# A four-layer model on one core: one table of constants, layer-1 weights made beside layer 0, and the first half batch sent ahead

## The chip, the core and the metric

The kernel runs on one core of a Trainium2 chip as one launch. The metric is the device time of one execution in microseconds; lower is better. Six names are used for the engines: PE is TensorE (matrix products into PSUM), DVE is VectorE, ACT is ScalarE, POOL is GpSimd, SP is SyncE, which issues the DMA transfers, and PEld is the weight load of PE.

## The reference

The input is `data`, 4 sequences of 1024 rows with 128 columns, all float32. Four pairs of an attention-like step and a feed-forward step follow one another, eight residual steps in all, and each is closed by a layer normalisation over the 128 columns. The sketch names the steps in the kernel's counting, layer 0 to layer 7.

```
x = data
x = ln(x + concat(x, softplus(count(x) @ W1 + b1)) @ W2)      # layer 0 (count: see below)
x = ln(x + gelu(x @ bin(w1).T + b1) @ bin(w2).T + b2)         # layer 1: bin(w) = row mean of |w| times sign(w)
x = ln(x + attn(x))                                           # layer 2: for each row and head, scores q[i]*k[j] of the row's own
                                                              #   64 channels, causal softmax over j, times v[j]
x = ln(x + ln2(gelu(x @ tern(W_fc).T)) @ tern(W_proj).T)      # layer 3: ternary weights
x = ln(x + gated linear attention along the sequence)         # layer 4
x = ln(x + experts weighed by a sigmoid)                      # layer 5
x = ln(x + chunked state-space scan)                          # layer 6
x = ln(x + two rounds of top-2 of 64 Kronecker experts)       # layer 7
```

In layer 0 the count of a row is the sum over all 1024 rows of its sequence of the positive part of the cosine similarity. Layer 2 has, for every row and each of 16 heads, a 64 by 64 causal softmax: this is most of the work.

## The kernel before, in words

The 4096 rows are cut into 8 blocks of 512 rows (`NG`, `TPG` tiles of 128 rows each); two blocks are one sequence. A block has its rows `x` and its transposed rows `xT`, which the layers update in place.

The instructions are written by Python generators, one for each piece of work. A generator yields the name of the engine on which its next instructions run and what they need (free tiles of some kind, a condition). The class `Order` holds a planned clock for each engine; it always takes the piece that can start first by these clocks, and among pieces within 0.05 us the one with the better rank (`URGE`: closing a unit, then `prepare`, then the chains a, b and c, then the rest, then the feed). The instructions are emitted in that order, and every engine executes its own in that order. The instructions of `start` are ahead of that; on an engine they may change places with the planned ones.

The rooms in SBUF are lists of tiles by kind (`room`): six tiles `a` of 512 columns, one `ha` and one `hc` of 2048 columns, and so on. PSUM has `acc`, two `kvr` and four `bg`.

- `start` loads constants and parameters into one tile `cst`, one transfer for each, the first two blocks of x, the layer-0 weight `w0`, three rows of biases, and `Wo`. From SP's side these are issued one after the other.
- `fold` (rank feed) loads six pieces of the layer-2 weights into tiles `a`, multiplies each on PE with the constant matrix `less`, and copies the result on ACT into `wq` and `wkv`.
- `chain_a` runs `front(0)`, `front(1)`, `ternarise`, and then for each group of tiles the layers 3, 4 and 5, with `front(b + 2)` behind the groups of a block. `front` of an even block runs `layer0` for that block and the next one together; `front(0)` also runs `binarise`, which makes the two layer-1 weights (absolute value on ACT, sums over rows on PE, sign on ACT, three products or sums on DVE) and stores them in DRAM. Then it runs `layer1` for its own block and sets row `ONE` of `xT` to one on POOL. That row carries the biases of layer 2; `ready2` then says that layer 2 may begin on that block.
- `layer0` normalises both blocks into the tile `nT` (kind `ha`); `count` then makes eight similarity products for a block (each block needs `nT` of both), reduces each on ACT, and computes the rest of the layer.
- `layer1` loads both weights from DRAM, makes four projections into a tile `ha`, one GELU (a table load on ACT before and after it), four sums over the hidden columns, and the normalisation.
- `prepare` makes, tile by tile, the queries and the running maxima and minima of the keys, and copies them by DMA into the layouts `qr` and `mr`. `feed` and `rest` are layer 2 itself: for each of 64 units of work 17 ring steps, each of them a product on DVE into a piece of the ring `ringe`, a subtraction on POOL, an exponential on ACT, a sum on PE, another product on DVE and another sum on PE. `close` finishes a unit.
- `chain_b` runs layer 6 and `chain_c` runs layer 7 on the groups that chain a has finished. How far a chain may lag behind the feed is told by `LAG`, in units of the feed's progress.

Of the kernel before, what the change touches and what calls it, by code (L numbers as in the profile page):

```python
# [20 lines left out]
P = 128  # L21
# [8 lines left out]
H, C, R, S, NK = 16, 64, 4, 2, 16  # L30
SH = S * H
ERING = 8768
LUMPS = 8
EPS = 0.05
ONE = 96
LAG = {"chain_a": (0.7, 300), "chain_b": (1.6, 290), "chain_c": (2.6, 132)}

# [248 lines left out]
class Model:  # L286
# [94 lines left out]

    def start(self):
        nc, a = self.nc, self.a
        load = {"ident": P, "rep": P, "SL": P, "U": P, "ex4": P, "ex2": P, "g4": 16, "g2": 32, "su": P, "sd": P, "par": 4, "iota": LUMPS,
                "blk": P, "less": P, "bz": 48, "route": 16, "beyond": R}
        par = {"f0_b1": 4, "f1_lnw": 4, "f1_lnb": 4, "a2_nw": 1, "f2_b1": 16, "f2_Wu": 1, "a0_W1": 1, "a0_b1": 1}
        wide = {"f2_bu": 1, "a3_bdt": 16, "a3_Alog": 16, "f3_sup": 1, "f3_sdn": 1}
        total = sum(load.values()) + sum(par.values()) + sum(wide.values()) + 64 + 32 + 128
        cst = self.keep([P, total], "cst")
        self.k, at = {}, 0  # L390

        def put(name, src, cols, bcast=False, rows=P):
            nonlocal at
            dst = cst[:, at : at + cols]
            self.k[name] = dst
            at += cols
            for r in range(0, P, rows):
                self.d.dma_start(dst[r : r + rows], src.to_broadcast([P, cols]) if bcast else src)

        put("ident", a["c_ident"], P)  # L400
        self.ident = self.k["ident"]
        self.ones = self.keep([P, P], "ones")
        self.v.memset(self.ones, 1.0)
        self.neghalf = self.keep([P, TPG], "neghalf")
        self.v.memset(self.neghalf, -0.5)
        self.eps = self.keep([P, 1], "eps")
        self.v.memset(self.eps, LN_EPS)
        for g in (0, 1):
            self.load_x(g)
        for n, c in par.items():  # L410
            put(n, a[n], c)
        for n, c in load.items():
            if n != "ident":
                put(n, a["c_" + n], c)
        for n, c in wide.items():
            put(n, a[n], c, bcast=True)
        put("bup", a["f3_bup"], 64, rows=64)
        put("bdn", a["f3_bdn"], 32, rows=32)
        put("bd", a["c_bd"], 128)
        self.w0 = self.keep([P, 2, D], "w0")  # L420
        self.d.dma_start(self.w0, a["a0_W2"].rearrange("(c p) d -> p c d", p=P))


        self.bias = self.keep([66, 512], "bias", dtype=BF16)
        self.v.memset(self.bias, 0.0)
        left, part = self.new("a"), self.new("b").bitcast(BF16)[:66, :512]
        self.v.memset(left[:66], 0.0)
        for i in range(3):
            self.d.dma_start(left[32 * i : 32 * i + 2], a["bias"])
        for i in range(3):  # L430
            self.v.tensor_copy(part, left[:66])
            self.v.tensor_copy(self.bias[32 * i : 32 * i + 2], part[32 * i : 32 * i + 2])
            self.v.tensor_tensor(left[:66], left[:66], part, ALU.subtract)
        self.drop(left, part)
        self.pick = self.keep([66, 2], "pick", dtype=BF16)
        self.v.tensor_copy(self.pick, self.k["rep"][:66, :2])
        self.Wo = self.keep([P, 8, D], "Wo")
        self.d.dma_start(self.Wo, a["a1_Wo"].rearrange("(c p) d -> p c d", p=P))
        self.lo0 = self.keep([P, 8, C], "lo0")
        self.g.memset(self.lo0, 0.0)  # L440
        self.g.memset(self.lo0[:, :, 0:1], -BIG)
        self.ering = Ring(self.keep([P, ERING], "ringe"), ERING)
        self.state = self.keep([P, H, 8], "state")
        self.last = self.keep([P, 8], "last")
        self.negA = self.keep([P, H], "negA")
        self.s.activation(self.negA, self.k["a3_Alog"], AF.Exp)
        self.v.tensor_scalar_mul(self.negA, self.negA, -1.0)

        self.ident16 = self.keep([P, P], "ident16", dtype=BF16)
        self.v.tensor_copy(self.ident16, self.ident)  # L450
        self.mask16 = self.keep([P, P], "mask16", dtype=BF16)
        self.v.tensor_scalar(self.mask16, self.k["SL"], -30000.0, None, ALU.mult)
        self.nbu = self.keep([P, 1], "nbu")
        self.v.tensor_scalar_mul(self.nbu, self.k["f2_bu"], -1.0)
# [150 lines left out]
        yield from self.norm(g, "a%d" % (g.k % 2), po)  # L605

    def layer0(self, b):
        gs = self.blocks[2 * b : 2 * b + 2]
        for g in gs:
            if g.x is None:  # L610
                yield "SP", self.free("x")
                self.load_x(g.k)
            yield "ACT", self.free("xT")
            g.xT = self.new("xT")
        yield "ACT", self.free("ha")
        nT = self.new("ha")
        yield from self.together(*(self.normalise(g, nT) for g in gs))
        yield from self.together(*(self.count(g, nT) for g in gs))
        self.drop(nT)


    def binarise(self):

        self.w1 = []
        for half, n, count in ((0, 1, D), (1, 4, 512)):
            src = self.a["f0_w1T"] if half == 0 else self.a["f0_w2T"].rearrange("(c p) d -> p c d", p=P)
            wT = yield from self.load("a", src, *((512,) if half == 0 else (4, D)))
            wT = wT if half == 0 else wT.rearrange("p c d -> p (c d)")
            cols = 512 // n
            yield "ACT", self.free("a", 3)  # L630
            ab, bw, alpha = self.new("a"), self.new("a"), self.new("a")
            self.s.activation(ab, wT, AF.Abs)
            yield "PE", self.free("bg")
            pa = self.new("bg")
            for i in range(n):
                self.pe.matmul(
                    pa[:, :cols], lhsT=self.ones, rhs=ab[:, i * cols : (i + 1) * cols], start=(i == 0), stop=(i == n - 1)
                )
            yield "ACT"
            self.s.activation(alpha[:, :cols], pa[:, :cols], AF.Copy, scale=1.0 / count)  # L640
            self.s.activation(bw, wT, AF.Sign)
            self.drop(pa)
            yield "DVE"
            for i in range(n):
                s = slice(i * cols, (i + 1) * cols)
                self.v.tensor_tensor(bw[:, s], bw[:, s], alpha[:, :cols], ALU.mult)
            self.v.tensor_tensor(bw, bw, wT, ALU.subtract)
            self.v.tensor_tensor(wT, wT, bw, ALU.add)
            self.drop(ab, bw, alpha)
            yield "SP"  # L650
            self.w1.append(self.keep([P, 512], "w1", pool=self.dram))
            self.d.dma_start(self.w1[half], wT)
            self.drop(wT)

    def project(self, out, lhsT, rhs, bias):
# [1053 lines left out]

    def front(self, b):  # L1710
        if b.k % 2 == 0:
            yield from self.layer0(b.k // 2)
        if b.k == 0:
            yield from self.binarise()
        yield from self.layer1(b)
        yield "POOL"
        self.g.memset(b.xT[ONE : ONE + 1], 1.0)
        self.ready2 = b.k + 1
# [59 lines left out]
    def run(self):  # L1778
# [13 lines left out]
        with self.tc.manual_schedule():  # L1792
            self.log_exp()
            self.order.spawn(self.fold(), "feed")
            self.order.spawn(self.prepare(), "prepare")
            for chain in (self.chain_a, self.chain_b, self.chain_c):
                self.order.spawn(chain(), chain.__name__)
            self.order.spawn(self.feed(), "feed")
            self.order.run()
# [13 lines left out]
def arrays_of(i):  # L1813
    f = {k: np.asarray(v) for k, v in i.items()}
    c = np.ascontiguousarray
    row = lambda v: c(np.reshape(v, (1, -1)))
    cols = lambda v: c(np.reshape(v, (-1, P)).T)
    a = {
        "x": c(f["L0_attn_data"].reshape(NB * SEQ, D)),
        "a0_W1": cols(f["L0_attn_W1"]),  # L1820
        "a0_b1": cols(f["L0_attn_b1"]),
        "a0_W2": f["L0_attn_W2"],
        "f0_w1T": c(f["L0_ffn_w1"].T),
        "f0_w2T": c(f["L0_ffn_w2"].T),
        "f0_b1": cols(f["L0_ffn_b1"]),
        "a1_Wo": f["L1_attn_Wo"],
# [50 lines left out]
    for n, s in (("up", "up"), ("dn", "down")):  # L1877
# [5 lines left out]
    p, q = np.arange(P)[:, None], np.arange(P)[None, :]  # L1883
# [1 line left out]
        "ident": p == q,  # L1885
        "SL": p > q,
        "U": p <= q,
        "rep": p % 32 == q % 32,
        "blk": (p % 16 == q % 16) / 8.0,
        "less": ((p == q) * 1.0 - (p == ONE)) * (q != ONE),  # L1890
        "bz": np.pad(p // 8 == np.arange(16)[None, :], ((0, 0), (16, 16))) * 8**-0.5,
# [9 lines left out]
        "par": np.concatenate([p // n % 2 == np.arange(2)[None, :] for n in (4, 2)], 1) * LUMPS,  # L1901
        "iota": np.arange(LUMPS)[None, :] + 0 * p,
    }
    a.update({"c_" + n: c(np.asarray(v, np.float32)) for n, v in k.items()})
    return a


# [15 lines left out]
```

## Time and profile before

| | |
|---|---|
| time, median of 3 runs (lowest, highest) | 4459.69 us (4457.38, 4463.85) |
| profiled execution, own time | 4459.83 us |
| its span, first to last instruction | 4458.1 us |
| mean granted PE clock | 0.875 |
| DVE busy | 3637.0 us, 82% of the span |
| PE busy | 3532.0 us, 79% |
| POOL busy | 2697.3 us, 61% |
| ACT busy | 2443.8 us, 55% |

The busy times are sums over instructions, and what an engine waits for comes from the events of the semaphores. Nearly every instruction of this kernel is recorded by one helper, so that they all have the line L52; they are told apart by their tiles. In the order of time, a row has the start, the time (of one instruction or of several alike that are merged, with their number behind an x), the engine, the operation, the tile written and those read, and in brackets how long the engine had been idle and what ended that. `SPq` is a transfer's issue on SP's queue. In the table by stage a row has the stretch and its length, the busy time (and number of instructions) of PE, PEld, DVE, ACT and POOL, the granted PE clock, the DMA engines' mean busy share, and GB/s. In the table of waits the numbers are the sum in us, how often, and the longest.

### The profile page before, as it was taken

The page shows a single profiled execution, that of the slowest core. Times are in us where ns is not written, and L with a number is a line of the kernel's source. Part 1 is how long each engine was busy: PE and PEld are TensorE (multiplying, and loading weights), DVE is VectorE, ACT ScalarE, POOL GpSimd, SP SyncE. Part 2 cuts the span into 40 slices and gives each one's busy share as a digit, 9 for nine tenths or more (in the row PEclk, how much of TensorE's full clock was granted, in tenths as well). Part 3 has the DMA queues.
Part 4 walks back from the last instruction along what each step waited for, and adds up shares of the span by engine and source line. Part 5 has one row for each costly group of instructions (what it writes and reads, how often), then busy time and mean ns, then how long its engine had stood idle before and what let it go on. Part 6 is the DMA issues. An engine that isn't in the chain of part 4 may idle for free.

```text
span 4458.1 us, 91232 instructions
## 1 busy us (share of the span) xinstructions
PE 3532.0 (79%) x37044; PEld 1856.1 (42%) x37044; DVE 3637.0 (82%) x5143; ACT 2443.8 (55%) x4083; POOL 2697.3 (61%) x1254
## 2 busy tenths in 40 slices
PE   4567677788788888888788888988788888879973
PEld 2222224344344434444354434544354434437762
DVE  2899999899888998879979998779989998883421
ACT  3455555766446755657555655657555654555520
POOL 0598866776567775567756766557666775560111
PEclk8788889988899989989899888999998988998976
DMA  1221212212223232222323333133323223331555
GB/s 52 67 57 39 47 42 61 50 44 50 58 65 79 73 95 67 67 72 67 96 64 86 77 87 84 38 84 87 89 60 96 67 74 86 77 89 34 142 153 124
DMA packets 389933, 328.12 MB, mean 74 GB/s; under 512 B 201660, under 2 KB 325372, under 8 KB 389512
## 3 DMA queue, kind: packets, MB, share of 16 engines
q1 hardware_dynamic: 379016, 288.73, 26.3%
q0 software_dynamic: 10496, 33.56, 2.6%
q8 instruction: 290, 4.75, 0.5%
q14 instruction: 131, 1.07, 0.1%
HBM read 147.05 MB, written 40.89 MB: 42 GB/s over the span
## 4 chain that ended last, share of the span: by engine, by line
DVE 37%; PE 31%; issue 12%; POOL 9%; ACT 9%; DMA 2%; SPq 1%; DVEq 0%; POOLq 0%; ACTq 0%
DVE ringe L52 23%; PE bg L52 18%; PE acc L52 10%; POOL ringe L52 9%; DVE bg L52 5%; ACT ringe L52 4%; PE kvr L52 3%; SPq L52 1%; DVE a L52 1%; DVE x L52 1%; ACT ha L52 1%; DVE b L52 1%; DVE ast L52 1%; DVE t L52 1%; ACT b L52 1%
## 5 line engine op out<-in xcount | busy, mean ns | idle before, releaser
L52 POOL TENSOR_TENSOR ringe<-ringe,mr 128x1024 f32<-128x1024 f32 (+14 forms) x1088 | 2548.7, 2380 | 1150.5 <-DVE ringe L52 789.9
L52 PE MATMUL acc<-ringe,cst 128*32 128x256 f32 (+6 forms) x17418 | 1370.6, 428 | 509.2 <-ACT ringe L52 244.3
L52 ACT ACTIVATE ringe<-ringe 128x256 f32<-128x256 f32 (+14 forms) x962 | 997.6, 1053 | 790.2 <-POOL ringe L52 788.1
L52 DVE TENSOR_TENSOR ringe<-ringe,kvr 128x1024 f32<-128x1024 f32 (+14 forms) x1098 | 1289.8, 1204 | 129.9 <-PE acc L52 108.2
L52 DVE TENSOR_TENSOR ringe<-qr,kvr 128x1024 f32<-128x1024 f32 (+14 forms) x1088 | 1278.4, 1211 | 82.3 <-PE acc L52 45.7
L52 PEld LDWEIGHTS acc<-ringe,cst 128*32 128x32 f32 x17418 | 424.5, 115 | 1230.7 <-DVE ringe L52 467.6
L52 ACT ACTIVATE ringe<-ringe,cst 128x256 f32<-128x256 f32 x512 | 353.5, 771 | 106.7 <-POOL ringe L52 106.1
L52 PE MATMUL bg<-xT,a 128*128 128x512 f32 (+2 forms) x506 | 286.9, 675 | 34.8 <-DVE t L52 11.1
L52 PEld LDWEIGHTS bg<-b,b 64*128 64x128 f32 (+1 forms) x1650 | 178.8, 203 | 101.3 <-issue 42.6
L52 PE MATMUL bg<-b,b 64*128 64x128 f32 (+2 forms) x1650 | 202.2, 290 | 18.9 <-DVE b L52 5.5
L52 PE MATMUL kvr<-wkv,xT 128*32 128x256 f32 x2048 | 157.1, 430 | 48.4 <-DVE ringe L52 48.0
L52 PE MATMUL bg<-a,ha 128*128 128x128 f32 x1168 | 169.5, 291 | 12.8 <-ACT ha L52 12.8
L52 DVE TENSOR_TENSOR_SCAN bg<-lo,bg 128x512 f32<-128x512 f32 x128 | 155.4, 1217 | 22.2 <-ACT bg L52 22.2
L52 ACT COPY b<-bg 128x512 f32<-128x512 f32 (+2 forms) x245 | 106.7, 446 | 121.7 <-PE bg L52 119.8
L52 PEld LDWEIGHTS bg<-a,ha 128*128 128x128 f32 x1168 | 149.9, 201 | 24.9 <-ACT ha L52 14.5
L52 PEld LDWEIGHTS bg<-xT,a 128*128 128x128 f32 (+1 forms) x506 | 92.1, 213 | 159.1 <-issue 62.0
L52 ACT ACTIVATE ha<-bg,cst 128x512 f32<-128x512 f32 (+1 forms) x157 | 102.2, 665 | 79.8 <-PE bg L52 78.2
L52 POOL DMA_INDIRECT c<-in_f_tdn,elumps x22 | 20.8, 943 | 200.4 <-issue 196.0
L52 ACT ACTIVATE bg<-bg 128x512 f32<-128x512 f32 (+3 forms) x176 | 89.2, 509 | 75.8 <-PE bg L52 73.3
L52 ACT ACTIVATE b<-cst,five 128x128 f32<-128x128 f32 x412 | 129.5, 392 | 0.0
L52 DVE TENSOR_TENSOR b<-b,bg 128x256 f32<-128x256 f32 (+3 forms) x272 | 100.9, 401 | 34.0 <-PE bg L52 18.3
L52 PE MATMUL bg<-b,cst 128*128 128x512 f32 (+1 forms) x208 | 113.9, 634 | 0.5 <-ACT b L52 0.4
(598 smaller groups left out, 4641.5 us busy)
## 6 DMA issues: line engine op xcount, KB each, us to landing
qr<-q SPq DMA_DIRECT2D x512, 128.0 KB
mr<-t SPq DMA_DIRECT2D x512, 128.0 KB
a<-in_f_W SPq DMA_DIRECT2D x65, 256.0 KB
c<-in_f_Wdn SPq DMA_DIRECT2D x55, 256.0 KB
tu<-c SPq DMA_DIRECT2D x52, 256.0 KB
c<-tu SPq DMA_DIRECT2D x200, 64.0 KB
c<-td SPq DMA_DIRECT2D x98, 128.0 KB
td<-c SPq DMA_DIRECT2D x47, 256.0 KB
```

The costliest lines, as they stand in the source:

```text
L52: return f(*args, **kw)
```

## The change

- All constants and the small parameters come as one array `cst` that is put together on the host, in the order of `CST`. It is loaded by two transfers: the identity alone, and the other 1475 columns. The two blocks of x are issued ahead of each. The parameters that were spread over the partitions by a broadcasting transfer are repeated in the array. The constant `rep` has 32 columns in place of 128.
- `binarise` is spawned as a task of its own with the rank of chain a, ahead of `prepare` and the chains. Every `front` waits, before `layer1`, until both stored weights are there.
- `layer0(0)` normalises both blocks into a tile `hc`, runs `count` for block 0 alone, and hands the tile on. `front(0)` then goes to `layer1`. `front(1)` runs `count` for block 1 with that tile, gives it back, and goes to `layer1`. For later pairs `layer0` does both blocks together as before, in `ha`.

```diff
+CST = {
+    "ident": P, "a0_W1": 1, "a0_b1": 1, "f0_b1": 4, "f1_lnw": 4, "f1_lnb": 4, "a2_nw": 1, "f2_b1": 16, "f2_Wu": 1,
+    "f2_bu": 1, "a3_bdt": 16, "a3_Alog": 16, "f3_sup": 1, "f3_sdn": 1, "bup": 64, "bdn": 32, "rep": 32, "SL": P, "U": P,
+    "ex4": P, "ex2": P, "g4": 16, "g2": 32, "su": P, "sd": P, "par": 4, "iota": LUMPS, "blk": P, "less": P, "bz": 48,
+    "route": 16, "beyond": R, "bd": P,
+}
...
     def start(self):
...
-        def put(name, src, cols, bcast=False, rows=P):
-            nonlocal at
-            dst = cst[:, at : at + cols]
-            self.k[name] = dst
+        cst = self.keep([P, sum(CST.values())], "cst")
+        self.k, at = {}, 0
+        for name, cols in CST.items():
+            self.k[name] = cst[:, at : at + cols]
             at += cols
-            for r in range(0, P, rows):
-                self.d.dma_start(dst[r : r + rows], src.to_broadcast([P, cols]) if bcast else src)
-
-        put("ident", a["c_ident"], P)
+        self.load_x(0)
+        self.d.dma_start(cst[:, :P], a["cst"][:, :P])
+        self.load_x(1)
+        self.d.dma_start(cst[:, P:], a["cst"][:, P:])
...
-        for g in (0, 1):
-            self.load_x(g)
-        for n, c in par.items():
-            put(n, a[n], c)
-        for n, c in load.items():
-            if n != "ident":
-                put(n, a["c_" + n], c)
-        for n, c in wide.items():
-            put(n, a[n], c, bcast=True)
-        put("bup", a["f3_bup"], 64, rows=64)
-        put("bdn", a["f3_bdn"], 32, rows=32)
-        put("bd", a["c_bd"], 128)
...
     def layer0(self, b):
+
+        room = "ha" if b else "hc"
...
-        yield "ACT", self.free("ha")
-        nT = self.new("ha")
+        yield "ACT", self.free(room)
+        nT = self.new(room)
         yield from self.together(*(self.normalise(g, nT) for g in gs))
+        if b == 0:
+            yield from self.count(gs[0], nT)
+            return nT
         yield from self.together(*(self.count(g, nT) for g in gs))
         self.drop(nT)
...
     def binarise(self):
 
-        self.w1 = []
...
-            self.w1.append(self.keep([P, 512], "w1", pool=self.dram))
-            self.d.dma_start(self.w1[half], wT)
+            put_by = self.keep([P, 512], "w1", pool=self.dram)
+            self.d.dma_start(put_by, wT)
+            self.w1.append(put_by)
             self.drop(wT)
...
     def front(self, b):
         if b.k % 2 == 0:
-            yield from self.layer0(b.k // 2)
-        if b.k == 0:
-            yield from self.binarise()
+            self.nT = yield from self.layer0(b.k // 2)
+        elif b.k == 1:
+            yield from self.count(b, self.nT)
+            self.drop(self.nT)
+        yield "SP", self.when(lambda: len(self.w1) == 2)
         yield from self.layer1(b)
...
             self.order.spawn(self.fold(), "feed")
+            self.w1 = []
+            self.order.spawn(self.binarise(), "chain_a")
             self.order.spawn(self.prepare(), "prepare")
```

On the host, `arrays_of` puts the constants and parameters together into `cst` and passes the single arrays no more.

More of the change, by code (lines that the diff above doesn't have):

```diff
@@ L383, in start @@
         nc, a = self.nc, self.a
[L384 to L389, printed above, removed]
+        cst = self.keep([P, sum(CST.values())], "cst")
         self.k, at = {}, 0
-        def put(name, src, cols, bcast=False, rows=P):
-            nonlocal at
-            dst = cst[:, at : at + cols]
-            self.k[name] = dst
+        for name, cols in CST.items():
+            self.k[name] = cst[:, at : at + cols]
             at += cols
-            for r in range(0, P, rows):
-                self.d.dma_start(dst[r : r + rows], src.to_broadcast([P, cols]) if bcast else src)
-        put("ident", a["c_ident"], P)
+        self.load_x(0)
+        self.d.dma_start(cst[:, :P], a["cst"][:, :P])
+        self.load_x(1)
+        self.d.dma_start(cst[:, P:], a["cst"][:, P:])
         self.ident = self.k["ident"]
@@ L1887, in arrays_of @@
         "U": p <= q,
-        "rep": p % 32 == q % 32,
+        "rep": p % 32 == q[:, :32],
         "blk": (p % 16 == q % 16) / 8.0,
@@ L1903, in arrays_of @@
     }
-    a.update({"c_" + n: c(np.asarray(v, np.float32)) for n, v in k.items()})
+    k.update({n: a.pop(n) for n in ("f0_b1", "f1_lnw", "f1_lnb", "a2_nw", "f2_b1", "a0_W1", "a0_b1", "f2_Wu")})
+    k.update({n: np.tile(a.pop(n), (P, 1)) for n in ("f2_bu", "a3_bdt", "a3_Alog", "f3_sup", "f3_sdn")})
+    k.update(bup=np.tile(a.pop("f3_bup"), (2, 1)), bdn=np.tile(a.pop("f3_bdn"), (4, 1)))
+    a["cst"] = np.concatenate([np.asarray(k[n], np.float32) for n in CST], 1)
     return a
```

## The prediction, made before the changed kernel ran

> **What bounds the kernel now.** I read the busy times of the page first, then the busy time by stage, then the order of time of the first 136 us, and last the waits of the long middle stage. The stages are cut where the work of the start changes:
>
> ```profile
> 0.00:26.00 26.00, 0.05 (x1) 0.06 (x1) 5.33 (x19) 2.78 (x10) 1.88 (x7) 1.00 0.39 100
> 26.00:69.00 43.00, 33.74 (x116) 18.88 (x116) 11.38 (x35) 24.91 (x71) 1.01 (x1) 0.91 0.09 31
> 69.00:88.00 19.00, 4.33 (x11) 2.46 (x12) 4.35 (x9) 3.12 (x7) 0.00 (x0) 0.50 0.21 59
> 88.00:110.00 22.00, 13.13 (x49) 8.76 (x50) 3.63 (x13) 8.31 (x10) 0.52 (x1) 0.73 0.09 33
> 110.00:136.00 26.00, 18.26 (x84) 9.27 (x83) 11.28 (x20) 10.08 (x13) 0.00 (x0) 0.83 0.48 109
> 136.00:500.00 364.00, 229.42 (x2490) 82.92 (x2494) 351.53 (x341) 187.24 (x227) 309.78 (x134) 0.80 0.21 48
> 500.00:4000.00 3500.00, 2891.95 (x29631) 1463.09 (x29623) 3113.28 (x4225) 2055.24 (x3334) 2332.54 (x1056) 0.90 0.29 72
> 4000.00:4458.00 458.00, 341.11 (x4677) 270.61 (x4669) 136.21 (x485) 152.14 (x413) 51.53 (x56) 0.77 0.43 110
> ```
>
> From 136 us on DVE is busy 351.5 of 364 us (97%), and 89% up to 4000 us: that is the attention feed, whose sums go through DVE, POOL, ACT and PE together. Ahead of it no engine is busy most of the time: DVE does 36 us of work in 136 us, POOL 3.4. So the head is a chain of waits, and the feed can't begin before it ends. Its links, in order of time:
>
> ```profile
> 0.74 0.40 SPq L52 DMA_DIRECT2D cst<-in_c_ident  x1
> ...
> 21.25 0.40 SPq L52 DMA_DIRECT2D Wo<-in_a_Wo  x1
> 25.95 5.01 PE L52 MATMUL bg<-a,cst 128*128 128x512 f32 x6 [25.95 <-DMA a<-in_a_Wq]
> ...
> 36.94 9.61 PE L52 MATMUL bg<-ha 128*128 128x512 f32 x22
> ...
> 68.47 0.58 ACT L52 COPY xT<-bg 128x512 f32<-128x512 f32 x1 [1.97 <-PE bg L52]
> 68.95 0.63 ACT L52 ACTIVATE a<-a 128x512 f32<-128x512 f32 x1
> ...
> 84.51 0.33 SPq L52 DMA_DIRECT2D w<-a  x1
> 84.96 3.26 SPq L52 DMA_DIRECT2D a<-w  x4
> ...
> 87.83 5.65 PE L52 MATMUL bg<-xT,a 128*128 128x512 f32 x8 [6.55 <-DMA a<-w]
> ...
> 109.07 0.52 POOL L52 MEMSET xT<- 1x512 f32 x1 [74.59 <-ACT xT L52]
> 109.64 3.78 PE L52 MATMUL bg<-wq,xT 128*128 128x512 f32 x4 [1.32 <-POOL xT L52]
> ...
> 135.42 1.22 DVE L52 TENSOR_TENSOR ringe<-qr,kvr 128x1024 f32<-128x1024 f32 x1 [0.19 <-DMA qr<-q]
> ```
>
> (1) SP issues constants until 19.77 us, so that the first raw attention weight lands at 25.95 us. (2) The fold of these weights is interleaved with the normalising of both blocks of the first batch, until the first similarity matmul at 36.94. (3) Both blocks go through layer 0; the second one's transposed rows are copied at 68.47 and done at 69.05. (4) The layer-1 weights are binarised, stored to DRAM, loaded again at 84.96, and the first projection starts at 87.83. (5) Block 0 goes through layer 1 until the ones row is set at 109.07. (6) Queries, maxima and copies to all row groups are made until the first ring tile at 135.42. The wait behind it in the middle stage is:
>
> ```profile
> DVE ringe L52 <- PE acc L52: 146.3, 110, 9.8
> ```
>
> 146 us in 3500 is small beside DVE's 3113 busy: the feed is held mostly by DVE itself.
>
> **What the Trainium skill says.** "DMA: Bandwidth & Descriptors", Rules for kernel authors, advises to coalesce many small transfers into one large one, since under 64 KB mostly overhead is paid. The trace agrees in its own way: SP starts a constant about every 0.476 us, 0.5 KB or 64 KB alike. "TensorE: Matmul & The Clock Gate", Part 1, says that the clock is halved after an idle window and comes back with sustained work. The trace agrees: the granted clock is 0.50 in the stretch from 69 to 88 us, where PE works 4.3 of 19 us, and the 512-column matmuls there take about 1 us, against 0.43 in the similarity stretch. So head work that is pulled together may run a little faster than I count.
>
> **The change part by part.**
>
> *Table of constants.* Between 0.74 and 19.77 us SP issues 40 transfers (38 of constants, 2 of x): 19.03 / 40 = 0.476 us each. 36 go, so SP reaches the attention weights 36 x 0.476 = 17.1 us earlier, at 21.70 - 17.1 = 4.6 us. Then bytes decide. Ahead of the first raw weight stand x twice (0.52 MB), the identity (0.06), the rest of the table (1475 columns x 512 B = 0.76), the layer-0 weight (0.13), Wo (0.52), the first binarise weight (0.26, its chain goes ahead of the fold) and the weight itself (0.26): 2.5 MB. In the stretch 20 to 30 us the DMA engines moved 228 GB/s at a busy share of 0.70, so 325 at full share: 7.7 to 11 us, plus 0.74 for the first issue and some 2 us of latency (x is issued at 1.20 and used at 4.08, 2.9 us with 0.8 us of transfer). That is 10.4 to 13.7; I take 12. Gain 25.95 - 12 = 14 us (12.3 to 15.5). The matrix that the fold multiplies with is in the second load, ahead of the weights, so it holds nothing. The fold itself and the normalising keep their 11 us.
>
> *First block ahead of the second.* From 36.94 to 69.05 us two blocks are counted, 32.1 us. One alone: its eight similarities are done when the count is summed at 44.73, 7.8 us; summing and four counter matmuls 1.3; and from the scale of the counter to the copied rows 56.69 to 69.05 = 12.4, measured on the second block. With hops 21.8 us. Gain 10 us (8 to 13). The room changes from ha to hc so that layer 1 can have ha while the second block still holds the normalised rows; hc is used by layer 7 alone, which is hundreds of us away, so this costs nothing.
>
> *Binarising beside layer 0.* From 69.05 to 87.83 us, 18.8 us, leave the path, the reload among them: its two loads now find weights stored long ago, and can be issued while SP is idle. The work itself remains: ACT 0.63 + 0.60 + 0.62 + 0.63 + 0.28 + 0.62 = 3.4 us, PE 4.2, DVE 4.5. PE and DVE have room in 26 to 69 us (33.7 and 11.4 of 43 busy); ACT sets the pace of the similarities (one each 0.86 us, of which 0.77 is ACT), so I give 3 us back. Gain 16 us (13 to 19). The wait on both stored weights at the head of every layer 1 moves no data; what stands behind it is only chain a of its own block.
>
> Sum: 14 + 10 + 16 = 40 us, first ring tile at 135.4 - 40 = 95 us.
>
> *Given back.* The second block's count and layer 1 come after block 0's layer 1. Until now its layer 1 filled the gaps of 110 to 136 us; now its count does: ACT 8 x 0.77 + 3.0 = 9.2 us against 10.1 busy there in all before, DVE 5.5 us against 14.7 idle. Its layer 1 (DVE 0.70 + 1.74 + 1.36 = 3.8 us) and a part of the count meet the feed, where DVE is 97% busy. Bounds 2 us (all but a bit hidden) and 12 us (both whole, and prepare held for 3 on ACT and PE); I take 6. The second block isn't needed before the ninth unit: 136 ring steps, at 134 POOL steps in 364 us some 370 us after the feed's start. What else ran there, the ternarising, keeps its place behind layer 1.
>
> *Does the shift reach the end?* The chains a, b and c are paced by the feed's progress, not by time, so what follows should move as one piece. The part from 4000 to 4458 us hangs on the feed's last tile (the last POOL subtraction starts at 3985.8). I take 1 to 1, with an unknown: the planner's order of the middle is made anew. The pace of equal stretches of 500 us varies from 123 to 154 ring steps (POOL subtractions on ring tiles) as the layers beside it differ; I allow 0.5% of 3865 us, 19 us, either way.
>
> Net 40 - 6 = 34 us. The profiled execution took 4459.83 us (span 4458.1 and 1.7 around it), the median of the runs is 4459.69, so there is nothing to convert: 4460 - 34 = 4426 us.
>
> **Rivals.**
>
> *A tile shortage eats a part.* There are six tiles of kind a. The fold asks for six, binarising for one and then three at once, each normalising for one. With SP fast, loads are issued before bias frees the sixth, and the normalising or the binarising may have to wait until the fold hands tiles back. If the binarise chain then ends after the first block's layer 0, up to its 16 us stay on the path: gain 34 - 16 = 18, 4442 us. For it: the second block's squares start only at 31.91 us now, though x was issued by 2.2 us. Against: six fold tiles turn over in 6 x 0.85 us, and 22 us follow.
>
> *Slower: the new order of the middle.* Place: 136 to 4000 us. The rows that follow the head are the same, but the planner chooses between tasks within 0.05 us of each other, and a second block that is late by some tens of us sets another interleaving, with PE sums later for DVE. Price: 1% of the 3865 us is 39 us. It decides from 34 / 3865 = 0.9%; at 1.5% the time is 4460 - 34 + 58 = 4484 us. For it: such waits already make 146 us. Against: pacing by progress holds the chains to the feed, and PE's share there is 83%.
>
> *No change to be seen.* The shift is consumed by a slower middle of 0.65 to 1.1%: about 4460 us.
>
> **How the numbers follow.** The forecast's own case (gain 24 to 50) has 0.67; the tile shortage or a partial loss with a gain of 9 to 24 has 0.17; no change 0.06; slower 0.10. Within 0.2%, 9 us, is about what a measurement of this kernel can tell from no change. So faster 0.84, same 0.06, slower 0.10. The terms give 33 to 47 in the head, less 2 to 12, so 21 to 45 net, 4415 to 4439; with 19 us either way 4396 to 4458. I cut the far end to 4455, which leaves out most of no change and all of slower.
>
> **What would show it.** Right: two transfers into the table; the first fold matmul at 10 to 14 us; binarising's matmuls ahead of the first block's copied rows; the first projection within 2 us of these rows, at about 45 us; the ones row at 65 to 70 and the first ring tile at 88 to 103 us; DVE over 94% in the 300 us that follow; the last POOL subtraction about 34 us before 3985.8. Wrong: the first projection waits for a load or a store (shortage); the first ring tile is early but the last subtraction isn't (the middle); or the tail after it is longer than 472 us.

## The result, and the profile after

The changed kernel took 4441.89 us (median of 7 runs, 4433.58 to 4450.60), the kernel before in the same comparison 4459.69 (7 runs, 4450.24 to 4469.28). The ratio is 0.9965 with a 95% interval of 0.9952 to 0.9978: 15.6 us less, between 9.8 and 21.4. That is faster and inside the range, but 18 us short of the 34 that were forecast. The profiled execution was the longest of the seven, 4450.60 us with a span of 4448.8, so readings near the end of its trace stand about 9 us worse than the median.

The table by stage after the change, cut at the new boundaries of the start (columns as in the table by stage before):

```profile
0.00:12.00 12.00, 0.46 (x1) 0.46 (x2) 4.82 (x18) 1.50 (x2) 0.83 (x6) 1.00 0.78 265
12.00:47.00 35.00, 26.31 (x83) 13.99 (x83) 10.68 (x29) 20.68 (x62) 2.05 (x2) 0.92 0.18 57
47.00:70.00 23.00, 14.14 (x49) 9.29 (x49) 3.63 (x13) 8.31 (x10) 0.52 (x1) 0.65 0.00 1
70.00:98.00 28.00, 21.38 (x83) 10.94 (x83) 13.55 (x27) 10.12 (x25) 0.00 (x0) 0.74 0.41 91
98.00:500.00 402.00, 258.25 (x2764) 98.08 (x2767) 382.05 (x381) 214.67 (x266) 339.70 (x148) 0.80 0.22 52
500.00:4000.00 3500.00, 2878.81 (x29678) 1468.40 (x29670) 3090.18 (x4188) 2030.63 (x3294) 2303.41 (x1042) 0.89 0.28 71
4000.00:4449.00 449.00, 341.72 (x4406) 270.08 (x4398) 133.68 (x491) 154.52 (x424) 51.67 (x56) 0.79 0.45 113
```

The head is 98 us long in place of 135. Its links, in order of time:

```profile
2.24 0.50 SPq L59 DMA_DIRECT2D cst<-in_cst  x1
...
11.54 8.42 PE L59 MATMUL bg<-a,cst 128*128 128x512 f32 x12 [11.54 <-DMA a<-in_a_Wq]
...
15.84 0.31 ACT L59 ACTIVATE a<-x 128x128 f32<-128x128 f32 x1
...
17.55 0.31 ACT L59 ACTIVATE a<-x 128x128 f32<-128x128 f32 x1
...
24.57 7.03 PE L59 MATMUL bg<-hc 128*128 128x512 f32 x16
...
46.02 0.58 ACT L59 COPY xT<-bg 128x512 f32<-128x512 f32 x1 [1.97 <-PE bg L59]
46.66 0.50 PEld L59 LDWEIGHTS bg<-xT,a 128*128 128x128 f32 x2 [0.97 <-ACT xT L59]
46.66 6.22 PE L59 MATMUL bg<-xT,a 128*128 128x512 f32 x8 [0.68 <-ACT xT L59]
...
69.25 0.52 POOL L59 MEMSET xT<- 1x512 f32 x1 [49.14 <-ACT xT L59]
...
97.96 8.59 DVE L59 TENSOR_TENSOR ringe<-qr,kvr 128x1024 f32<-128x1024 f32 x10
```

The second and last load of the table is issued at 2.24 us. The first fold matmul starts at 11.54, in the 10 to 14 that were named. The squares of the first block start at 15.84 and those of the second at 17.55. The first projection of layer 1 starts 0.06 us after the copy of the first block's rows (46.02 + 0.58): it waits for these rows and for no weight. The ones row is set at 69.25 and the first ring tile is made at 97.96. From there DVE is busy 382 of 402 us, 95%. So the signs that were named for the head came true, and most of the loss lies behind it.

To find it, I used a yardstick that every trace of this kernel has: the 1088 POOL subtractions on ring tiles, one for each ring step. The start of the k-th one is read in two traces and subtracted. Negative is earlier than before, in us:

| ring step | 0 | 34 | 68 | 136 | 408 | 544 | 612 | 816 | 1087 (last) | span |
|---|---|---|---|---|---|---|---|---|---|---|
| start in the kernel before | 136.8 | 237.2 | 326.6 | 508.3 | 1446.3 | 1973.5 | 2198.4 | 3007.1 | 3985.8 | 4458.1 |
| changed kernel | -37.5 | -29.8 | -27.7 | -29.2 | -40.4 | -1.2 | +14.3 | -3.3 | -8.8 | -9.2 |

37.5 us are gained at the first step and 27.7 are left at step 68. That much still stands at step 136. Between steps 408 and 612 it all goes, and only a part comes back. The last subtraction is 9 us early where 34 were said.

### The profile page after: what moved, and what is told of

Its sections match the earlier page's. It is cut to its first block, busy times and chain, and to the rows that moved or that the text cites. A ratio compares the mean times of both kernels' runs of the same rounds, so it can differ in the third digit from the quotient of the medians.

```text
span 4448.8 us, 91173 instructions
## 1 busy us (share of the span) xinstructions
PE 3541.1 (80%) x37044; PEld 1871.2 (42%) x37044; DVE 3638.6 (82%) x5143; ACT 2440.4 (55%) x4083; POOL 2698.2 (61%) x1254
## 3 DMA queue, kind: packets, MB, share of 16 engines
q1 hardware_dynamic: 374488, 288.68, 26.4%
## 5 line engine op out<-in xcount | busy, mean ns | idle before, releaser
L59 PE MATMUL acc<-ringe,cst 128*32 128x224 f32 (+7 forms) x17420 | 1355.8, 426 | 506.7 <-ACT ringe L59 247.2
L59 ACT ACTIVATE ringe<-ringe 128x512 f32<-128x512 f32 (+14 forms) x964 | 998.9, 1052 | 784.4 <-POOL ringe L59 781.5
L59 PE MATMUL bg<-xT,a 128*128 128x512 f32 (+2 forms) x494 | 279.1, 676 | 28.6 <-DVE ha L59 5.4
L59 PEld LDWEIGHTS bg<-b,b 128*128 128x128 f32 (+1 forms) x1614 | 182.4, 215 | 105.0 <-issue 44.9
L59 PE MATMUL bg<-b,b 128*128 128x8 f32 (+2 forms) x1614 | 205.3, 303 | 14.2 <-DVE b L59 7.5
L59 PE MATMUL kvr<-wkv,xT 128*32 128x256 f32 x2048 | 164.7, 448 | 41.9 <-DVE ringe L59 41.9
L59 DVE TENSOR_TENSOR_SCAN bg<-lo,bg 128x512 f32<-128x512 f32 x128 | 155.3, 1217 | 33.8 <-ACT bg L59 33.7
L59 DVE TENSOR_TENSOR b<-b,bg 128x256 f32<-128x256 f32 (+2 forms) x274 | 101.5, 400 | 31.5 <-PE bg L59 14.5
L59 ACT ACTIVATE bg<-bg 128x512 f32<-128x512 f32 (+4 forms) x180 | 90.0, 502 | 60.6 <-PE bg L59 57.3
L59 PEld LDWEIGHTS kvr<-wkv,xT 128*32 128x32 f32 x2048 | 60.9, 122 | 129.7 <-DVE ringe L59 83.7
```

Source lines behind the costliest of these rows:

```text
L59: return f(*args, **kw)
```

## The experiments

The edits are shown against the kernel before or the changed one. Kernels e1 to e4 ran on one chip, e5 to e8 on a second, e9 to e12 on a third, e13 and e14 on a fourth, each beside runs of the kernel before; times are compared within a chip. The chip of the result's comparison is not on record. A gain in us is the ratio's distance from 1 times the median of the kernel before there, with the interval's half width. Two theories stood first: that the part which sends the first block ahead gives back what it gains (at once, or by another order of the middle), and that only a part of any shift of the head reaches the end.

### The parts apart: e1, e2, e7, e8

e1 is the changed kernel without its third part: `layer0(0)` does both blocks together in `ha`, as before, and `front` no longer counts the second block by itself (those lines are left out here).

```diff
     def layer0(self, b):
-        room = "ha" if b else "hc"
+        room = "ha"
...
-        if b == 0:
-            yield from self.count(gs[0], nT)
-            return nT
         yield from self.together(*(self.count(g, nT) for g in gs))
```

> The changed kernel without its third part: table in two loads and binarising beside layer 0, but both blocks of the first batch go through layer 0 together. Behind the head (the last 19536 of 19612 PE and 5064 of 5127 DVE instructions) it emits the same instructions in the same order as the kernel before. Theory A (the head start is carried to the end, and what was lost is lost by the other order of the middle that the third part brings): first ring tile 27 us earlier (14 + 16 less a few), the distance to the kernel before stays at 24 to 30 us at every ring step, time 4432 us, ratio 0.9935 to 0.9945. Theory B (an earlier feed loses about half of its start to the engines whatever the order): the distance shrinks along the middle to 13 us, ratio 0.997.

Measured: 4439.05 us (6 runs) against 4461.41 (27), ratio 0.9947 (0.9927 to 0.9966): 23.6 ± 9 us faster.

e2 is the kernel before with the third part alone. Its lines in `layer0` are those of the change and are left out here.

```diff
     def front(self, b):
         if b.k % 2 == 0:
-            yield from self.layer0(b.k // 2)
+            self.nT = yield from self.layer0(b.k // 2)
+        elif b.k == 1:
+            yield from self.count(b, self.nT)
+            self.drop(self.nT)
```

> The third part alone: the first block goes through layer 0 and layer 1 ahead of the second; constants and binarising as before. Behind the head its order is that of the changed kernel (the last 19560 of 19612 PE instructions). Theory A: first ring tile 8 to 10 us earlier, some 7 of it given back in the first ring steps, then the changed order costs its 20 us: slower than before by 10 to 20 us, ratio 1.002 to 1.0045. Theory B: a small gain, 2 to 5 us, ratio 0.999.

Measured: 4463.16 us (22 runs), ratio 1.0004 (0.9995 to 1.0013): 1.8 ± 4 us slower, no difference that shows. Both theories missed it: one said 10 to 20 us slower, the other 2 to 5 us faster.

e7 has the table alone, e8 the binarising beside layer 0 alone (the task of its own and the wait in `front`), each in one run. Of the edit of e8:

```diff
...
-        if b.k == 0:
-            yield from self.binarise()
+        yield "SP", self.when(lambda: len(self.w1) == 2)
...
+            self.w1 = []
+            self.order.spawn(self.binarise(), "chain_a")
...
```

> The table in two loads alone, the rest as before; the order behind the head is that of the kernel before. First ring tile 12 to 16 us earlier than 135.4 us (the first raw attention weight at 10.4 to 13.7 us in place of 25.95, partly eaten by the bias rows that hold the sixth tile a), and the distance stays along the middle. Theory A on the single time: 4446 us within the spread of single runs of 12 us.

> Binarising as a task of its own alone, the rest as before; the order behind the head is that of the kernel before (POOL's order whole). First ring tile 13 to 19 us earlier than 135.4 us, and the distance stays along the middle. Theory A on the single time: 4444 us within the spread of single runs of 12 us.

Measured: 4450.29 and 4443.81 us, beside 4460.30 for the kernel before (7 runs, 4457.80 to 4470.34). The first ring tile on DVE, in order of time, in e7, e8 and e2:

```profile
121.66 1.22 DVE L58 TENSOR_TENSOR ringe<-qr,kvr 128x1024 f32<-128x1024 f32 x1 [0.19 <-DMA qr<-q]
```

```profile
117.59 1.22 DVE L52 TENSOR_TENSOR ringe<-qr,kvr 128x1024 f32<-128x1024 f32 x1 [0.19 <-DMA qr<-q]
```

```profile
125.17 8.59 DVE L52 TENSOR_TENSOR ringe<-qr,kvr 128x1024 f32<-128x1024 f32 x10
```

Against 135.42 us these are gains of 13.8, 17.8 and 10.3 us: the sum's terms of 14, 16 and 10, each measured by itself. What becomes of them is the next table.

| distance to the kernel before at step | 0 | 34 | 68 | 408 | 544 | 612 | 1087 |
|---|---|---|---|---|---|---|---|
| e7, table | -13.8 | -13.7 | -13.7 | -22.7 | -20.8 | -20.7 | -22.2 |
| e8, binarising | -17.8 | -18.2 | -18.2 | -20.5 | -18.1 | -18.1 | -21.6 |
| e1, both | -29.8 | -30.2 | -30.0 | -38.7 | -36.8 | -36.8 | -38.2 |
| e2, first block ahead | -10.3 | -3.5 | -1.5 | -17.3 | +22.0 | +37.4 | +14.3 |

Two things follow. The first two parts are kept whole, and e1 has the gain without the third part. The third part gives back 8.8 of its 10.3 us within 68 steps, and then shows the same loss between steps 408 and 612 as the changed kernel. In the traces of the kernel before, e7, e8 and e1 the instructions behind the head stand in the same order on DVE, ACT and POOL. The changed kernel and e2 share another one. So the loss goes with the order, and it is the third part that changes it.

The tables end at the last ring step, and the times do not. e2 is 14.3 us late there in its trace, and yet its time is that of the kernel before: its end follows after 455.0 us, that of the kernel before after 472.3. This tail comes up again at the close.

The give-back can be read in the first 34 ring steps. The table by stage of the kernel before and then of the changed one:

```profile
136.80:237.20 100.40, 56.27 (x584) 18.35 (x584) 94.39 (x93) 45.91 (x53) 79.84 (x35) 0.77 0.21 50
```

```profile
99.30:207.40 108.10, 67.06 (x628) 25.44 (x628) 98.13 (x104) 52.93 (x62) 80.39 (x35) 0.73 0.24 57
```

and what DVE waited for there (us in total, times, longest), before and changed:

```profile
DVE ringe L52 <- PE acc L52: 4.1, 6, 1.5
```

```profile
DVE ringe L59 <- PE acc L59: 8.9, 6, 3.2
```

The same 34 steps take 108.1 us in place of 100.4. DVE does 3.7 us more, about the 3.8 that the second block's layer 1 was said to bring there. It waits 4.8 us longer for sums on PE, where the second block's products now stand between the ring's: 67.1 us busy in place of 56.3. The granted PE clock is a little lower there too, 0.73 against 0.77; what each of the two adds to the wait was not parted.

### Does a shift of the head reach the end: e5, e6

A chain of 40 small loads into the same column, each waiting for the last, is put into `start` ahead of the constants; the planner isn't told of it, so that the order behind stays. In e6 it loads a column of the table. e5 is the kernel before with it, e6 the changed kernel.

```diff
+        for _ in range(40):
+            nc.sync.dma_start(cst[:, 0:1], a["a0_W1"])
```

> The kernel before with a chain of 40 tiny transfers into one column of the constants ahead of its other loads, each waiting for the one before it, which the planner isn't told of: the same work in the same order on PE, ACT and POOL, with a head that is some 70 to 95 us longer in which the engines idle. Theory A (what moves the head moves the end by as much, with the same order): the time grows by what the first ring tile is late, within 8 us. Theory C (a shift of the head reaches the end only to about 70%, because a chip that has idled more is granted a faster PE clock later, which the first four runs leave possible: 23.6 of 30, some 17 of 26, some 11 to 17 of 26 us): it grows by 0.6 to 0.8 of that, and the granted clock from 200 us on is higher by some thousandths than in the kernel before.

> The changed kernel with the same chain of 40 tiny transfers ahead of its loads, the order unchanged. Theory A: the time grows, against the changed kernel's 4442 us, by what the first ring tile is later than its 98 us, within 8 us. Theory C: by 0.6 to 0.8 of that.

Measured: e5 4516.45 us (4 runs) against 4460.30 (7), ratio 1.0125 (1.0109 to 1.0142), 55.8 ± 7.4 us slower; its first ring tile came 60.2 us late. e6 4512.96 us (4 runs), 1.0117 (1.0098 to 1.0136), 52.2 ± 8.5 us slower. In e5 the ring steps are late by 60.2 at step 0, 60.3 at 68, 56.8 at 544 and 53.4 at the last. So an unchanged order carries a shift nearly whole. The faster clock that theory C supposed is there by 0.004 in the one trace of e5 (0.883 from 200 us on, 0.879 in the kernel before), and over whole executions it does not show: 0.872 to 0.876 in e5's four, 0.873 to 0.878 in the kernel before's seven. e6 is late by 26.4 us at step 0 and 36.3 at step 68, but 62.9 at 544, 78.4 at 612 and 51.8 at the last. Against the changed kernel itself its distance is 63.9, 64.0, 64.1, 64.1 and 60.6: the loss in the middle is there again at a head that is 64 us later. It does not come from when the feed starts.

### Another order for all: e3, e4, e9 to e12

The planner takes pieces within `EPS` of each other by rank. With 0.06 in place of 0.05 all variants get one common order behind the head, and with 0.07 again one, another.

```diff
-EPS = 0.05
+EPS = 0.06
```

This edit was made to the kernel before (e3), the changed kernel (e4), e1 (e9) and e2 (e10); with 0.07 to the kernel before (e11) and the changed kernel (e12).

> The kernel before with the planner's tolerance EPS at 0.06 in place of 0.05: same work, another order of the middle. Theory A: the order of the middle is worth tens of us by itself, so this moves by more than 15 us, either way, with the same head (first ring tile at 135 us within 1). Theory B: the middle is held by the engines' work, so within 8 us of before, ratio 0.998 to 1.002.

> The changed kernel with EPS 0.06. With this tolerance both kernels emit the same order behind the head (the last 18907 of 19612 PE and 4874 of 5127 DVE instructions are the same). Theory A: 28 to 32 us less than the kernel before with EPS 0.06 (37.5 in the head less some 7 given back in the first ring steps), and this distance holds from ring step 68 to the end. Theory B: 13 to 18 us less, the distance shrinking along the middle.

> Table and binarising beside, without the third part, with EPS 0.06: behind the head the order is that of the kernel before with EPS 0.06 (the last 19536 of 19612 PE instructions). Theory A: first ring tile 29 us earlier than that kernel's 134.7, nothing given back in the first 68 ring steps, and the distance holds to the end: 4387 - 29 = 4358 us, ratio 0.9765, with an order-free reason to be a little below the changed kernel with EPS 0.06 (26 us at ring step 68). A theory D, that the third part is worth its 10 us of head to the end, expects it 8 us slower than that one.

> The third part alone with EPS 0.06, in the same order of the middle as the kernel before with EPS 0.06 (only the head and its neighbourhood differ). Theory A: first ring tile 10 us earlier, 8 to 9 us given back by ring step 68, so within 5 us of that kernel's 4387 us, ratio 0.982 to 0.984. Theory D: 10 us below it, 4377 us, ratio 0.981.

> The kernel before with EPS 0.07: a third order of the middle, same head. Theory A: another time again, more than 15 us from the 4387 us of EPS 0.06, with the first ring tile at 135 us within 1.

> The changed kernel with EPS 0.07, which behind the head emits the order of the kernel before with EPS 0.07 (the last 18705 of 19612 PE instructions). Theory A: first ring tile 36 us earlier than there, 9 to 10 us given back by ring step 68, and 26 us kept to the end, within the 10 us of five runs each. Theory B: the distance shrinks along the middle to 13 us.

| | us (runs) | kernel before there | ratio (95%) |
|---|---|---|---|
| e3, before, 0.06 | 4386.78 (5) | 4461.41 (27) | 0.9828 (0.9805 to 0.9851) |
| e4, changed, 0.06 | 4371.42 (5) | 4461.41 | 0.9804 (0.9786 to 0.9823) |
| e9, e1's parts, 0.06 | 4402.08 (5) | 4480.04 (11) | 0.9830 (0.9814 to 0.9846) |
| e10, e2's part, 0.06 | 4440.20 (6) | 4480.04 | 0.9907 (0.9892 to 0.9921) |
| e11, before, 0.07 | 4453.84 (6) | 4480.04 | 0.9938 (0.9924 to 0.9952) |
| e12, changed, 0.07 | 4417.95 (4) | 4480.04 | 0.9870 (0.9854 to 0.9886) |

The order is worth more than the change: one digit of a planner's constant makes the kernel before 77 us faster (e3), by no gain in the head, where its first ring tile is at 134.7 us. In its trace 38.3 us of the gain stand at the last ring step, and the tail is 20 us shorter. With one order for both, neither loses against the other between steps 408 and 612 (against the kernel before e3 loses 50 us there and has them back by step 816): e4 is ahead of e3 by 26.1 us at step 68, 28.6 at 612, 41.7 at the last; e12 is ahead of e11 by 31.6, 33.8 and 37.3. In time e12 is 30.5 ± 9.5 us ahead of e11. e4 is ahead of e3 by only 11 ± 13, which alone would settle nothing. e9 against e10, 32.5 us apart at step 68, differ by 34.5 ± 9.6 in time.

Two times do not fit what was expected. e9 was to be 29 us faster than e3 and has the same ratio; e10 was to be level with it, and gains 42 ± 7 us where e3 gains 77 ± 10. Up to the last ring step both traces are as expected: e9 is 28.3 us ahead of e3 at step 68 and 29.8 at the last one, e10 4.1 and 4.9 us behind. The misfit lies in the tails, 493.3 and 494.0 us from the last subtraction to the end in e9 and e10, 452.1 in e3. What differs there is shown at the close.

e4 is the fastest version measured: 2.0% below the kernel before and 1.6% below the changed one.

### The changed head with the old order: e13, e14

e13 is the changed kernel in which the pieces behind `front(1)` are taken in the order that the kernel before has, from a list in the file; the extra wait of `front` is kept for the first two blocks alone. e14 is the changed kernel itself, beside it on the same chip.

```diff
+    def as_before(self, ready):
+        place = {}
+        for t in ready:
+            at = OLD.get(t.key, [])
+            place[t] = at[t.steps] if t.steps < len(at) else 0
+        return min(ready, key=place.get)
...
+            if self.old:
+                self.step(self.as_before([p[1] for p in starts]))
+                continue
```

> The changed kernel, whole, whose planner takes its pieces behind the second block's front in the order in which the kernel before took them (that order is written into the file as a list); work and head are those of the changed kernel. Theory A (order): first ring tile at 98 us, 28 us ahead of before at ring step 68, and that distance is still there at the last ring step (within 8), where the changed kernel in its own order had 9 left. Time: 22 to 30 us below before on the same chip, ratio 0.9935 to 0.995, 5 to 15 us below the changed kernel beside it. Theory E (the loss belongs to the changed head itself, for example to tiles and phases it leaves behind, and not to the order): within 3 us of the changed kernel beside it, and the distance shrinks along the middle.

> The changed kernel as it is, on the same chip as the partner of the run with the old order. Theory A: ratio 0.996 to 0.9975 to before, its distance at the last ring step 5 to 15 us; slower than its partner by 5 to 15 us. Theory E: the two within 3 us.

Measured: e13 4450.90 us (5 runs) against 4474.42 (12), ratio 0.9945 (0.9932 to 0.9959), 24.6 ± 6 us faster. e14 4483.66 us (8 runs), 1.0016 (1.0000 to 1.0031): on this chip the changed kernel is not faster at all. The ratios differ by 0.0071 ± 0.0021, so the order alone costs 32 ± 9 us here. That is more than the 5 to 15 us that were expected. Part of it goes with a lower clock: the granted clock is 0.868 in the mean of e14's eight executions and 0.874 in that of e13's five. Whether the order lowers it on this chip was not parted; in e2, with the same order on another chip, it was 0.877 beside 0.875 in the kernel before. By ring steps, with the kernel before's as zero:

| step | 0 | 68 | 408 | 544 | 612 | 816 | 1087 |
|---|---|---|---|---|---|---|---|
| e13, old order | -38.4 | -30.9 | -32.6 | -30.4 | -27.4 | -25.1 | -28.5 |
| e14, its own order | -35.8 | -25.9 | -37.1 | +10.4 | +26.2 | +12.4 | +13.5 |

The table by stage has it as work done in the same 3500 us from 500 us on, in e13 and then in e14:

```profile
500.00:4000.00 3500.00, 2894.62 (x29509) 1473.61 (x29510) 3094.08 (x4225) 2054.17 (x3361) 2301.98 (x1041) 0.90 0.28 71
```

```profile
500.00:4000.00 3500.00, 2886.95 (x29242) 1475.14 (x29242) 3078.12 (x4161) 2023.24 (x3277) 2304.67 (x1042) 0.88 0.28 70
```

In e13 DVE does 16 us more of work (3094.1 against 3078.1) in the same time. Where the changed kernel loses most are the 34 ring steps from 510 to 544. The table by stage of that stretch, in e13 and then in e14:

```profile
1789.00:1943.20 154.20, 130.91 (x1156) 71.42 (x1160) 119.95 (x197) 95.38 (x194) 89.74 (x47) 0.86 0.31 79
```

```profile
1782.90:1983.90 201.00, 168.72 (x1528) 97.69 (x1527) 139.67 (x250) 118.88 (x241) 89.96 (x45) 0.89 0.23 62
```

It is the same picture in the kernel before and then in the changed one:

```profile
1820.00:1974.00 154.00, 131.49 (x1160) 71.66 (x1160) 119.88 (x196) 94.79 (x194) 89.76 (x46) 0.86 0.31 79
```

```profile
1774.00:1972.00 198.00, 165.90 (x1530) 96.52 (x1530) 139.54 (x250) 118.83 (x241) 89.89 (x45) 0.90 0.24 63
```

They take 198 us in place of 154. The same holds for every trace, on whatever chip: 153.9 to 154.2 us in the six with the old order (kernel before, e1, e5, e7, e8, e13), 198.0 to 201.0 in the four with the new one (changed, e2, e6, e14). The clock is not the reason: it is higher in the slower stretch in both pairs, 0.90 against 0.86 and 0.89 against 0.86. Of DVE's work there 81.1 us are on ring tiles before and 85.1 after (the same view for these tiles alone). The rest, of the layers beside the feed, is 38.8 before and 54.4 after, and DVE is idle 34.1 and 58.5. Of the 44 us, 16 are work of other layers that fell into this stretch and is missing elsewhere, so that its time can come back; 24 are idle time.

## Why the prediction was off: point by point

*Table of constants*: right. e7 gains 13.8 us where 14 was said, and in the changed kernel the first fold matmul lies at 11.54 where 12 was.

*Binarising beside layer 0*: right, 17.8 us in e8 for 16 (13 to 19).

*First block ahead of the second*: right as a term of the head, 10.3 us in e2 for 10.

*Sum of the head*: 37.5 us for 40. Singly the parts make 41.9. Together 4.4 are lost: from the first fold matmul to the first similarity product passes 13.0 us (11.54 to 24.57) in place of 11.0 (25.95 to 36.94); one ACT operation of the binarising (0.64 us at 22.48) and two of its PE sums (1.13 us at 23.17) now lie in that stretch. Another part lies between the first projection and the first ring tile, 51.3 us in place of 47.6. The causes of the two were not parted.

*Given back*: right in kind, 9.8 us by step 68 for the 6 that I took out of 2 to 12. e1 gives back nothing (29.8 to 30.0), e2 8.8 of 10.3. The working counted DVE's extra work (3.7 measured) and left out that PE's extra work delays the sums that DVE waits for (4.8). So before the order comes in, the third part is worth 1.5 us by e2 and costs 2.3 by the changed kernel beside e1 (27.7 and 30.0 us ahead at step 68). Up to here 6 of the missing 18 us are explained: 34 said, 27.7 there at step 68.

*Does the shift reach the end?* **This is the step that failed.** It has two halves. "1 to 1" nearly holds for an unchanged order. The pairs with one order are e1, e5 and e13 against the kernel before, e9 against e10, e12 against e11, e4 against e3. They were apart by 30.0, 60.3, 30.9, 32.5, 31.6 and 26.1 us at step 68, and by 23.6 ± 9, 55.8 ± 7.4, 24.6 ± 6, 34.5 ± 9.6, 30.5 ± 9.5 and 11 ± 13 in time. A line through zero, weighted by these intervals, has a slope of 0.89 (0.80 to 0.97). So a tenth may be lost on the way, and a carry under 0.8 does not fit.

The other half, "0.5% either way" for the order made anew, put its cost at zero in the mean and gave no reason for it. That is the term that was off. From 27.7 us at step 68, 24.6 would be left at a slope of 0.89. 15.6 ± 5.8 were, so that the new order takes some 9 us in the comparison of the result, 12 if the slope is 1. With what the head and the give-back lost, that makes up the missing 18. In four comparisons the new order costs, in us:

| | lost from step 68 to the last, in the trace | in time |
|---|---|---|
| changed kernel, result | 18.9 | 9 to 12, ± 6 |
| e2 | 15.8 | 3 ± 4 |
| e6 | 15.5 | 16 to 20, ± 8.5 |
| e14, in time against e13 | 39.4 | 32 ± 9 |

The loss up to the last ring step shows in all four; the traces with the old order (e1, e5, e7, e8, e13) move between 8.5 us of gain and 2.4 of loss over the same steps. (The changed kernel's trace is its slowest execution, 9 us above the median, so its 18.9 may be high.) The price in time is less certain, since the tail behind differs from trace to trace: e2's doesn't stand clear of zero, and the 32 us are 0.8% of the 3865 us and outside the 19 that were allowed. What an order can do in all, e3 shows: 77 us, 1.7%.

*The rivals*. "A tile shortage" named 4442 us, the measured time within 0.2 us, and yet its mechanism isn't there: the first projection waits for no weight, and the second block's squares start at 17.55 us and not at 31.91. A time that fits proves no cause. "Slower: the new order of the middle" had the mechanism. Its place, 136 to 4000 us, and its reason, another interleaving from the late second block, are what e2, e13 and e14 show. The sign that it named, PE sums later for DVE, is a weak one: that wait is

```profile
DVE ringe L59 <- PE acc L59: 156.0, 118, 6.5
```

in the waits from 500 to 4000 us, 10 us more than the 146.3 before (beside e13 it is 20 more, 164.5 in e14 and 144.1 in e13). The price was what decided: 34 us were needed to lose the gain. In the comparison of the result the order took 9 to 12, beside e13 32, where nothing of the gain was left. By the order alone e11 and e3 differ from the kernel before by 0.6 and 1.7%, 28 and 77 us, so the 19 us that were allowed were too few and the range was too narrow. Both were faster, so they would not have told that this order would be a slower one. That the measured time lies in the range is in part luck: "No change to be seen" is what e14 gave with the same kernel.

*The tail* after the last subtraction, which was to be longer than 472 us if the prediction were wrong, is 471.8. That it agrees so well may be chance, since over all 16 traces it takes 452.1 to 495.8 us.

What stays open is why one order is worse. That it is the order, and where it loses, is shown. Which of its pieces does it was not tried.

## What to carry to other kernels

Where a list scheduler makes the order of the instructions, a change of the head is two changes: the shift, which an engine-bound middle hands on nearly whole, and a new draw of the order, which here moved the time by some 3 to 77 us. Part them before believing either: hold the order fixed, or compare both kernels under a few values of the tie-break, and follow a repeated instruction, the k-th in one trace against the k-th in the other. And a late second stream can pay twice, as here, with its own work on the busy engine and with the delay that it causes to the sums for which that engine waits.

## What was unexpected of the hardware

The same two kernels compared differently in two places. Changed against before was 0.9965 (0.9952 to 0.9978) in the result and 1.0016 (1.0000 to 1.0031) beside e13. The medians of the kernel before were 4459.69 us in the result and 4461.41, 4460.30, 4480.04 and 4474.42 on the four chips of the experiments. Much of the difference can lie in the tail, which takes 452.1 to 495.8 us in the 16 traces. In the five shortest (e3, e4, e2, e11, e12; up to 459.5 us) the granted PE clock of the tail is 0.81 to 0.84, in the five longest (e7, e1, e9, e10, e13; from 484.9 us) 0.75 to 0.78. It isn't the chip alone: e9 to e12 ran on one, and e11 and e12 took 458.4 and 459.5 us there, e9 and e10 493.3 and 494.0. Nor is it the order alone: e4 and e9 have the same one there, and from the last subtraction to the end they took 452.8 and 493.3 us. Some 16 of these 40 us are one wait. The same instruction of DVE in e4 and then in e9, in order of time:

```profile
4087.20 0.42 DVE L59 TENSOR_TENSOR a<-ha,bg 128x256 f32<-128x256 f32 x1 [0.99 <-PE bg L59]
```

```profile
4124.93 0.42 DVE L58 TENSOR_TENSOR a<-ha,bg 128x256 f32<-128x256 f32 x1 [17.30 <-remote]
```

In e3 it stands 0.99 us, in e10 17.2. In all four POOL sends out 16 indirect transfers at this time, one every 1.25 us; in e9 and e10 DVE goes on 3 us after the last of them is out, in e3 and e4 in their midst. What it waited for isn't shown ("remote" is a release for which the trace has no instruction). PE then stands 15.8 us too, and the clock falls. The table by stage in e9, of the later part of the wait and of the 28.6 us behind it:

```profile
4113.90:4125.30 11.40, 0.00 (x0) 0.00 (x0) 0.37 (x2) 0.37 (x1) 6.09 (x7) 0.50 1.13 342
```

```profile
4125.40:4154.00 28.60, 26.49 (x108) 22.21 (x107) 9.45 (x45) 6.03 (x17) 0.00 (x0) 0.50 0.97 261
```

"TensorE: Matmul & The Clock Gate" of the Trainium skill, Part 1, ties a halved clock to a window of idleness, and this trace agrees: the clock (the first figure after POOL's) is 1.00 until PE has stood for 4 us and 0.50 from there. But work doesn't bring it back soon: PE is busy for 26.5 of the next 28.6 us at 0.50, and 1.00 is granted only from 4175 us on, 50 us after the wait. The table by stage from 200 to 250 us behind the last subtraction, in e4 and then in e9, shows the difference:

```profile
4105.80:4155.80 50.00, 40.89 (x884) 34.22 (x883) 15.29 (x42) 9.68 (x26) 0.00 (x0) 0.77 0.72 191
```

```profile
4117.70:4167.70 50.00, 34.77 (x291) 29.00 (x293) 14.38 (x57) 7.27 (x21) 3.20 (x4) 0.50 0.78 217
```

PE gets through 884 and 291 matmuls in the 50 us. Each trace is one execution: it says how large the effect can be and not why. The 27 executions of the kernel before beside e1 have something of it too: the longer ones have the lower clock (4446.20 us at 0.882, 4477.61 at 0.873, a correlation of -0.83), and which follows which isn't shown.
The chain of small loads in e6 (in order of time; the rows alike are merged):

```profile
14.72 54.70 SPq L397 DMA_DIRECT2D cst<-in_cst  x34
```

34 loads of 0.5 KB that each wait for the last took 54.7 us, 1.6 us each, where independent ones were issued every 0.476 us: waiting for each costs three times what issuing the next does.
